# Two places in the order of a long fused kernel: when the sampling weights are loaded, and where a depthwise unit's closing activation stands

## The chip, the cores and the metric

The kernel runs on one core of one Trainium2 chip. The metric is the device time of one execution in microseconds (us). Of three runs of the kernel before, the median is 9661.97 us (9661.39 to 9698.82). The engines are TensorE (PE, with its weight loads as PEld), VectorE (DVE), ScalarE (ACT), GpSimd (POOL) and SyncE (SP, whose only work here is to issue DMAs).

## What is computed

The input is 32 images of 96 channels and 56 x 56 pixels, in float32. Two layers follow each other.

Layer 0 is an inverted bottleneck with quantised weights: a 1x1 convolution to 576 hidden channels, a 3x3 depthwise convolution, squeeze and excite, and a 1x1 convolution back to 96 channels, plus the input:

```python
h = silu(bn(conv1x1(x, fake_quant(w1)), g1, b1, m1, v1))
h = silu(bn(depthwise3x3(h, fake_quant(w2)), g2, b2, m2, v2))
pooled = mean(h, axis=(2, 3))
s = sigmoid(silu(pooled @ se_w1 + se_b1) @ se_w2 + se_b2)
x = x + bn(conv1x1(h * s, fake_quant(w3)), g3, b3, m3, v3)
```

Layer 1 attends and samples. It weighs its input by channel and by pixel from 2-D Fourier magnitudes, predicts nine offsets and a gate for each pixel by 3x3 convolutions, samples the weighted image bilinearly at the nine moved places, and normalises over the batch:

```python
y = x * ca * sa                              # from |rfft2(x)| and the mean and norm over channels
aux = concat([y, coord, resize(mean(|rfft2(y)|))])
offset, gate = conv3x3(aux), sigmoid(conv1x1(relu(conv3x3(aux))))
y_base = conv3x3(y)
sampled = bilinear(y, grid + offset)         # nine places a pixel, 0 outside
z = (1 - gate) * y_base + gate * einsum(sampled, def_w)
out = relu(batchnorm(z) + x)                 # statistics over all 32 images
```

## The kernel before

**The stages.** `layers` carries three things at once. The main loop goes over the 32 x 7 bands of layer 1 (a band is eight rows of an image; `bands`, L1073), and each band over two halves `h`. Beside it run two generators that belong to later images: `second` (`attend`, the end of layer 0 and the attention of layer 1 for the image after) and `first` (`hidden`, layer 0's expansion and depthwise part for the image after that). `pump` (L1012) is called between groups of matmuls and moves the generators on, each at a pace that brings it to its end with the image. There are seven pumps in a half and three more at a band's end. Work that is to follow later is put into the list `later` with the slot at which it is due.

**A depthwise unit.** `hidden` (L203) works on nine units of an image (`UNITS`: 128 hidden channels by half an image each). TensorE and ACT expand the unit after (L168, L172) while DVE runs the nine taps of this one into the accumulator `acch` (L259 for the first, L261 for the eight others). `acch` has two buffers. `finish` (L218) is the unit's end: a Silu with batchnorm as scale and bias, in place, which also sums over the pixels into `pooled` (L221), and a store of the result to `h2d` in DRAM from ACT's queue (L223). In the text `finish` of a unit is called after the fourth tap of the next unit (`n == 3`, L263). Unit 8's is put off with `defer` (L270): it becomes due with a flush when the image's generators are drained, right behind its last tap. The result is read back by `project_loads` (L305) for the projection matmuls L323 and L329.

**Sampling.** For each band `offsets` (a generator, moved on once before the halves and then at each pump) makes the offsets, stores them to DRAM (`od`, L655), loads them spread over the positions of a small neighbourhood (`ht`, L667, on SP), turns them into bilinear hat weights on ACT (L670, L671) and stores these (`hd`, L674, on ACT's queue). That is done two bands ahead. Each half of a band needs a weight tile, the product of a column part and a row part of `hd`. `weights_load` (L678) reads the two parts into `wc` (three buffers) and `wr` (two buffers) by four broadcasting DMAs of 252 KB each on SP, and `weights` (L690) multiplies them on DVE (L692). `sample_tiles` (L713) then multiplies blocks of the image (`yt`, made by `block_channels`, L696) with these weights on TensorE (L721), and ACT evicts the results into `v` (L725); `pack` moves a part of `v` to other partitions (L732), and `deform` is the convolution with `def_w` (L740).

In a half, the text has the order: `prepare` (the loads, L1117), the first group of samples with three pumps, the ends of the half before, the product of the weights for the next half (L1131), the second group with four pumps, `pack`. `prepare(upto)` issues loads until `upto` halves have theirs, as far as `hds` reaches. So a weight tile's loads are issued at the top of the half whose middle holds its product, and the tile is used in the half after that.

**What sets the order.** The instructions are written in one text, and a planner orders each engine's instructions ahead of time: it plays the program with estimated durations and puts an instruction into its engine's order when its inputs are there in that play. At run time an engine works its order from front to back and waits where an input is late. SP is left out of the planner (`manual_schedule`, L1351): its DMAs are issued in the order of the text. `tc.keep_in_program_order(ins)` gives the planner one more edge: `ins` comes after the instruction that the text has just before it on the same engine. It concerns the order alone and adds no wait. It is used once in the kernel before, at L670.

Of the kernel before, what the change touches and what calls it, by code (L numbers as in the profile page):

```python
# [9 lines left out]
AF = mybir.ActivationFunctionType  # L10
# [54 lines left out]
AHEAD = 1  # L65
READY = 1
# [50 lines left out]
def bank(p):  # L117
    return p["mm"].tile([128, 512], FP, name="mm")
# [33 lines left out]
def expand(nc, p, xts, unit):  # L152


    w = p["w0"]
    ch, half = unit
    h1 = p["hp"][p["n_hp"] % len(p["hp"])]
    p["n_hp"] += 1
    p["h1"] = h1
    inv, sh = w["inv1"][:, ch : ch + 1], w["sh1"][:, ch : ch + 1]  # L160
    w1 = w["w1"][:, ch * 128 : min(HID, ch * 128 + 128)]

    def piece(parts, row0, rows):

        pt = bank(p)
        for p0, hf in parts:
            r0 = row0 - 1 + hf
            nc.tensor.matmul(pt[p0 : p0 + w1.shape[1], : rows * W], w1, xts[hf][:, r0 * W : (r0 + rows) * W],  # L168
                             start=True, stop=True)
        lo = parts[0][0]  # L170
        hi = parts[-1][0] + w1.shape[1]
        nc.scalar.activation(h1[lo:hi, row0 : row0 + rows, 1 : 1 + W],  # L172
                             pt[lo:hi, : rows * W].rearrange("p (h w) -> p h w", h=rows), AF.Silu,
                             bias=sh[lo:hi], scale=inv[lo:hi])

    if half is None:
        nc.vector.memset(h1[:64, 0, :], 0.0)
        nc.vector.memset(h1[64:, HH + 1, :], 0.0)
        for r in range(1, HH + 1, ER):
            piece([(0, 0), (64, 1)], r, ER)  # L180
            yield
        piece([(0, 0)], HH + 1, 1)
        piece([(64, 1)], 0, 1)
        yield
    else:
        r = 1 - half
        for rows in (ER + 1, ER, ER, ER):
            piece([(0, half)], r, rows)
            r += rows
            yield  # L190
# [12 lines left out]
def hidden(tc, p, x, xn, h2d, pooled, defer):  # L203


    nc = tc.nc
    w = p["w0"]

    def rows_of(x, half):
        xt = p["xt"].tile([C, (HH + 1) * W], FP, name="xt")  # L210
        r0 = half * (HH - 1)
        nc.sync.dma_start(xt, x[:, r0 : r0 + HH + 1].rearrange("c h w -> c (h w)"))
        return xt

    xts = p.pop("xts", None) or [rows_of(x, 0), rows_of(x, 1)]
    for _ in expand(nc, p, xts, UNITS[0]):
        yield
    def finish(u, acc):  # L218
        ch = UNITS[u][0]
        flat = acc.rearrange("p h w -> p (h w)")  # L220
        nc.scalar.activation(flat, flat, AF.Silu, bias=w["sh2"][:, ch : ch + 1], scale=w["inv2"][:, ch : ch + 1],  # L221
                             accum_out=pooled[:, u : u + 1])
        nc.scalar.dma_start(h2d[u], flat)  # L223

    before = None
    for u, (ch, half) in enumerate(UNITS):
        h1 = p["h1"]
        more = expand(nc, p, xts, UNITS[u + 1]) if u + 1 < len(UNITS) else iter(())
        if xn is not None and u in (5, 8):

            p.setdefault("xts", []).append(rows_of(xn, int(u == 8)))
        acc = p["acch"].tile([128, HH, W], FP, name="acch")

        rows_of_tap = lambda dy: (int(half == 0 and dy == 0), HH - int(half == 1 and dy == 2))
        diag = p.get("diag")
        taps = [k for k in (4, 0, 1, 2, 3, 5, 6, 7, 8) if diag is None or k not in TPE]
        parts = []
        if diag is not None:
            for r0 in range(0, HH, ER):
                pt = bank(p)[:, :EW].rearrange("p (h w) -> p h w", h=ER)  # L240
                for i, k in enumerate(TPE):
                    dy, dx = divmod(k, 3)
                    lo, hi = rows_of_tap(dy)
                    lo, hi = max(r0, lo), min(r0 + ER, hi)
                    nc.tensor.matmul(pt[:, lo - r0 : hi - r0], diag[:, ch, i], h1[:, dy + lo : dy + hi, dx : dx + W],
                                     start=(i == 0), stop=(i == len(TPE) - 1))
                parts.append((slice(r0, r0 + ER), pt))
            next(more, None)
            yield
        for n, k in enumerate(taps):  # L250
            dy, dx = divmod(k, 3)
            lo, hi = rows_of_tap(dy)
            win = h1[:, dy + lo : dy + hi, dx : dx + W]
            wk = w["w2"][:, ch, k : k + 1]
            if n == 0:
                for rs, pt in parts:
                    nc.vector.scalar_tensor_tensor(acc[:, rs], win[:, rs], wk, pt, ALU.mult, ALU.add)
                if not parts:
                    nc.vector.tensor_scalar(acc, win, wk, None, ALU.mult)  # L259
            else:  # L260
                nc.vector.scalar_tensor_tensor(acc[:, lo:hi], win, wk, acc[:, lo:hi], ALU.mult, ALU.add)  # L261
            if n % 2:
                if n == 3 and before:  # L263
                    finish(u - 1, before)
                next(more, None)
                yield
        for _ in more:
            pass
        before = acc
    defer(lambda: finish(len(UNITS) - 1, before))  # L270


# [405 lines left out]
def weights_load(nc, p, hd, h):  # L678

    src = hd.rearrange("n i t k -> n i (t k)")[:, :, h * NTH * KP : (h + 1) * NTH * KP]  # L680
    wc = p["wc"].tile([2 * NS, NTH * KP], FP, name="wc")
    wr = p["wr"].tile([2 * NS, NTH * KP], FP, name="wr")
    for s in range(2):
        ps = slice(s * NS, (s + 1) * NS)
        nc.sync.dma_start(wc[ps], src[2 * s].unsqueeze(0).to_broadcast([SB, SB, NTH * KP]))
        nc.sync.dma_start(wr[ps], src[2 * s + 1].unsqueeze(1).to_broadcast([SB, SB, NTH * KP]))
    return wc, wr
# [251 lines left out]
def layers(tc, a, dp, x1d, zd, stats, far):  # L939
# [6 lines left out]
    nc = tc.nc  # L946
    B = x1d.shape[0]
    with ExitStack() as ctx:
# [143 lines left out]
        def prepare(upto):  # L1092

            nonlocal n_loads
            while n_loads < min(upto, 2 * len(hds)):
                n, m = divmod(n_loads, 2)
                loads.append(weights_load(nc, p, hds[n], m))
                n_loads += 1
# [6 lines left out]
        for n, (b, j) in enumerate(bands):  # L1105
            if j == 0:
                st = p["st"].tile([C, NBD, 6], FP, name="st")
            if j == turn:
                drain()
                refill(b + 1, j * RB - PD)  # L1110
                flush()
                start(b + 1, slots)
            more = find(n + 2) if n + 2 < len(bands) else iter(())
            next(more, None)
            for h in range(2):
                v = p["vp"].tile([128, NTAP, NTH, 2, TP], FP, name="v")
                prepare(2 * n + h + READY + AHEAD)  # L1117
                s = ready.pop(0)
                yt = yts.pop(0)
                for i, group in enumerate(GROUPS):  # L1120
                    sample_tiles(nc, p, yt, s, v, group)
                    for _ in range(group[0][0], group[-1][1]):
                        next(more, None)
                        pump()
                    if i == 0:
                        for end in ends:
                            end()
                        ends.clear()
                        if h == 1 and n + 1 < len(bands):
                            yts.append(block_channels(nc, p, yp, bands[n + 1][1], 0))  # L1130
                        ready.extend(weights(nc, *ws) for ws in loads[:1])  # L1131
                        del loads[:1]
                        if h == 0:
                            yts.append(block_channels(nc, p, yp, j, 1))
                pack(nc, v)
                if h == 0:
                    if n % 2 == 0:
                        gates.extend(gates_of(nc, p, hids[n // 2]))
                    gate = gates.pop(0)
                ends.append(lambda n=n, h=h, v=v, gate=gate, st=st: end_half(n, h, v, gate, st))  # L1140
            for _ in more:
                pass
            pump()
            pump()
            pump()
            if b + 1 < B:
                refill(b + 1, (j + 1) * RB - PD if j < NBD - 1 else H)
            if j == NBD - 1:
                nc.vector.tensor_reduce(top[:, NBD:], top, AX.X, ALU.max)
# [350 lines left out]
```

## Time and profile before

| | us |
|---|---|
| median of three runs | 9661.97 |
| profiled execution | 9648.5 |
| its span, first to last instruction | 9646.7 |
| PE busy | 8472.7 (88%) |
| DVE busy | 7227.2 (75%) |
| ACT busy | 5322.1 (55%) |
| POOL busy | 2532.6 (26%) |
| taps of the depthwise units on DVE (L261) | 4320.5 in 2250 instructions |
| products of the weights on DVE (L692) | 564.6 in 448 instructions |
| closing activations on ACT (L221) | 487.5 in 288 instructions |
| mean granted clock of TensorE | 0.923 |

The profile is one execution taken by the hardware profiler. A line of a group gives line, engine, operation, tiles (out<-in) and shapes. A line of the waits reads "who <- for whom: total us, times, longest". A line of the timeline gives start, duration, engine (with a q: its queue, which issues DMAs), line, operation, tiles, count, and in square brackets the engine's idle time before it with what ended it. A line of a table of windows gives the window, its length, the busy time and count of each engine, the clock that was granted to TensorE (1 is full speed), the share of the DMA engines' time and GB/s.

### The profile page before, as it was taken

How to read it: one execution, taken by the hardware profiler on the slowest of the kernel's cores; microseconds unless marked ns; L12 is line 12 of the kernel's file. 1: busy time of each engine (PE TensorE's matmuls, PEld its weight loads, DVE VectorE, ACT ScalarE, POOL GpSimd, SP SyncE). 2: the span in 40 equal slices, each digit the busy share in tenths (PEclk: the TensorE clock that was granted, in tenths of full speed). 3: DMA queues.
4: the chain of work that ended last, by engine and by line, in shares of the span. 5: the costliest groups of instructions: out<-in, count | busy, mean ns of one | idle time of the engine just before them, and what ended most of it. 6: DMA issues, size and time to landing. Idle time of an engine off the chain costs nothing. (4 is left out here: it accounts for less than half of the span.)

```text
span 9646.7 us, 129705 instructions
## 1 busy us (share of the span) xinstructions
PE 8472.7 (88%) x48374; PEld 5064.2 (52%) x48374; DVE 7227.2 (75%) x6948; ACT 5322.1 (55%) x10262; POOL 2532.6 (26%) x2642
## 2 busy tenths in 40 slices
PE   6889989998999999999899989999999999999870
PEld 3455555555555555555555555555555555555540
DVE  7688777778777787877777887777878777777323
ACT  2355555565555556555555655555555555565453
POOL 1123223222222322222232322233222323322210
PEclk9899999999999999999999999999999999999985
DMA  2355555555555555555555555555555555554449
GB/s 94 95 143 148 151 152 160 150 149 143 147 155 154 160 154 145 145 149 155 154 160 155 145 142 153 151 158 154 153 139 145 150 157 157 153 152 135 130 154 417
DMA packets 1069473, 1485.98 MB, mean 154 GB/s; under 512 B 590438, under 2 KB 840086, under 8 KB 1056550
## 3 DMA queue, kind: packets, MB, share of 16 engines
q1 hardware_dynamic: 858747, 985.20, 37.9%
q10 hardware_dynamic: 153803, 329.80, 9.2%
q0 software_dynamic: 56288, 162.60, 6.7%
q8 instruction: 388, 6.36, 0.3%
q14 instruction: 247, 2.02, 0.1%
HBM read 1064.29 MB, written 412.65 MB: 153 GB/s over the span
## 5 line engine op out<-in xcount | busy, mean ns | idle before, releaser
L261 DVE SCALAR_TENSOR_TENSOR acch<-hp,w,acch 128x1512 f32<-128x1512 f32 (+1 forms) x2250 | 4320.5, 1920 | 32.8
L605 PE MATMUL mm<-yp,c_jointW 104*128 104x448 f32 x4032 | 1649.0, 561 | 9.0 <-ACT yt L709 5.5
L740 PE MATMUL pd<-v,c_def 128*96 128x224 f32 (+1 forms) x6272 | 1414.8, 376 | 127.6 <-ACT v L732 104.1
L703 POOL COPY ybl<-yp 96x448 f32<-96x448 f32 x896 | 1014.7, 1159 | 1903.7 <-PE mm L707 1903.3
L721 PE MATMUL mm<-wc,yt 64*96 64x144 f32 x12544 | 1168.1, 308 | 153.5 <-DVE yb L638 76.8
L740 PEld LDWEIGHTS pd<-v,c_def 128*96 128x96 f32 (+1 forms) x6272 | 1051.8, 173 | 437.4 <-ACT v L732 142.5
L168 PE MATMUL mm<-xt,w 96*128 96x392 f32 (+3 forms) x2688 | 1136.3, 561 | 133.8 <-ACT yt L709 96.0
L605 PEld LDWEIGHTS mm<-yp,c_jointW 104*128 104x128 f32 x4032 | 783.6, 196 | 806.0 <-issue 762.6
L721 PEld LDWEIGHTS mm<-wc,yt 64*96 64x96 f32 x12544 | 884.2, 167 | 489.8 <-issue 188.0
L221 ACT ACTIVATE acch<-acch,sh,inv 128x1568 f32<-128x1568 f32 x288 | 487.5, 1693 | 1159.0 <-DVE acch L261 1143.9
L692 DVE TENSOR_TENSOR wc<-wc,wr 128x1008 f32<-128x1008 f32 x448 | 564.6, 1260 | 704.2 <-DMA wr<-hd 690.5
L725 ACT COPY v<-mm 96x288 f32<-96x288 f32 (+1 forms) x2688 | 1003.6, 442 | 117.7 <-PE mm L721 78.9
L172 ACT ACTIVATE hp<-mm,sh,inv 128x392 f32<-128x392 f32 (+2 forms) x1216 | 811.8, 672 | 326.9 <-PE mm L168 282.1
L633 PE MATMUL mm<-yp,c_base0W 96*64 96x448 f32 x4032 | 913.5, 550 | 0.0
L323 PE MATMUL mm<-hq,w3s 128*96 128x392 f32 x2048 | 788.2, 531 | 127.4 <-DMA hq<-h2d 125.9
L655 POOL DMA_DIRECT2D od<-at x224 | 186.3, 832 | 2275.1 <-DVE at L651 1451.9
L732 ACT COPY v<-v 32x448 f32<-32x448 f32 x1344 | 755.3, 562 | 30.3
L168 PEld LDWEIGHTS mm<-xt,w 96*128 96x128 f32 (+1 forms) x2688 | 389.9, 189 | 495.1 <-issue 264.8
L709 ACT COPY yt<-mm 128x384 f32<-128x384 f32 (+1 forms) x896 | 350.9, 441 | 491.5 <-PE mm L707 489.4
L323 PEld LDWEIGHTS mm<-hq,w3s 128*96 128x96 f32 x2048 | 336.3, 173 | 477.7 <-issue 382.5
L466 POOL TENSOR_TENSOR o<-o,xc 96x392 f32<-96x392 f32 x256 | 396.5, 1549 | 643.9 <-ACT o L333 642.3
L633 PEld LDWEIGHTS mm<-yp,c_base0W 96*64 96x64 f32 x4032 | 294.6, 134 | 515.5 <-issue 490.2
(194 smaller groups left out, 9023.7 us busy)
## 6 DMA issues: line engine op xcount, KB each, us to landing
h2d<-acch ACTq DMA_DIRECT2D x288, 784.0 KB
wc<-hd SPq DMA_DIRECT2D x896, 252.0 KB
wr<-hd SPq DMA_DIRECT2D x896, 252.0 KB
hq<-h2d SPq DMA_DIRECT2D x128, 980.0 KB
hq<-h2d SPq DMA_DIRECT2D x128, 784.0 KB
x<-x1d SPq DMA_DIRECT2D x768, 98.0 KB
ht<-od SPq DMA_DIRECT2D x224, 252.0 KB
hd<-ht ACTq DMA_DIRECT2D x224, 252.0 KB
```

What stands on the lines that cost most here:

```text
L168: nc.tensor.matmul(pt[p0 : p0 + w1.shape[1], : rows * W], w1, xts[hf][:, r0 * W : (r0 + rows) * W], start=True, stop=True)
L172: nc.scalar.activation(h1[lo:hi, row0 : row0 + rows, 1 : 1 + W], pt[lo:hi, : rows * W].rearrange("p (h w) -> p h w", h=rows), AF.Silu, bia ...
L261: nc.vector.scalar_tensor_tensor(acc[:, lo:hi], win, wk, acc[:, lo:hi], ALU.mult, ALU.add)
L323: nc.tensor.matmul(pts[half][:C, :EW], w3s[:, ch], hq, start=(i == 0), stop=False)
L605: nc.tensor.matmul(view, weights[:, k], yp[:channels, r0 : r0 + RB, dx + PD - 1 : dx + PD - 1 + W], start=(k == 0), stop=(k == NTAP - 1))
L633: nc.tensor.matmul(pb[k % 2 * BC : (k % 2 + 1) * BC, :BW].rearrange("p (h w) -> p h w", h=RB), w["base"][:, k], yp[:C, r0 : r0 + RB, dx + ...
L692: nc.vector.tensor_tensor(wc, wc, wr, ALU.mult)
L703: nc.gpsimd.tensor_copy(yb[:, :, s], blocks)
L721: nc.tensor.matmul(pt[k][:C, (t - lo) * KP : (t - lo + 1) * KP], yt[ps, t], s[ps, t * KP : (t + 1) * KP], start=True, stop=True)
L725: nc.scalar.copy(v[:C, :, lo:hi, k].rearrange("c k t p -> c t k p"), pt[k][:C, : (hi - lo) * KP].rearrange("c (t k p) -> c t k p", t=hi - ...
L732: nc.scalar.copy(v[C:, 1 + 2 * i : 3 + 2 * i], v[i * QC : (i + 1) * QC, KA:])
L740: nc.tensor.matmul(out.rearrange("c q (t x) -> c t q x", x=TS), p["w"]["def"][ks, k], v[ks, k].rearrange("c t s (r x) -> c t (s r) x", r=T ...
```

## The change

The closing activation of a depthwise unit (L221) is wrapped in `tc.keep_in_program_order`. And `prepare`, which issues the loads of the weights, moves from the top of a half to just behind the product of the weights in its middle, with an argument that is larger by one: a weight tile's four loads are now issued half a half ahead of where they were, behind the product of the tile before it. The instructions themselves, the buffers and their sizes are the same.

```diff
     def finish(u, acc):
         ch = UNITS[u][0]
         flat = acc.rearrange("p h w -> p (h w)")
-        nc.scalar.activation(flat, flat, AF.Silu, bias=w["sh2"][:, ch : ch + 1], scale=w["inv2"][:, ch : ch + 1],
-                             accum_out=pooled[:, u : u + 1])
+        tc.keep_in_program_order(nc.scalar.activation(
+            flat, flat, AF.Silu, bias=w["sh2"][:, ch : ch + 1], scale=w["inv2"][:, ch : ch + 1], accum_out=pooled[:, u : u + 1]))
         nc.scalar.dma_start(h2d[u], flat)
...
             for h in range(2):
                 v = p["vp"].tile([128, NTAP, NTH, 2, TP], FP, name="v")
-                prepare(2 * n + h + READY + AHEAD)
                 s = ready.pop(0)
                 yt = yts.pop(0)
                 for i, group in enumerate(GROUPS):
...
                         ready.extend(weights(nc, *ws) for ws in loads[:1])
                         del loads[:1]
+                        prepare(2 * n + h + 1 + READY + AHEAD)
                         if h == 0:
                             yts.append(block_channels(nc, p, yp, j, 1))
```

## The prediction

> **What bounds the kernel now.** I read the page's busy shares first, then a table of windows over the long middle stage, then the waits, then the timeline around one wait of each kind.
>
> ```profile
> PE 8472.7 (88%) x48374; PEld 5064.2 (52%) x48374; DVE 7227.2 (75%) x6948; ACT 5322.1 (55%) x10262; POOL 2532.6 (26%) x2642
> ...
> 480.00:9120.00 8640.00, 7923.65 (x45735) 4738.19 (x45738) 6739.73 (x6242) 4956.84 (x9646) 2441.68 (x2507) 0.94 0.54 150
> ...
> ACT acch L221 <- DVE acch L261: 1143.9, 185, 12.7
> ...
> DVE wc L692 <- DMA wr<-hd: 690.5, 152, 18.3
> ...
> PE mm L323 <- DMA hq<-h2d: 125.9, 31, 9.4
> ...
> PE pd L740 <- ACT v L732: 104.1, 84, 5.4
> ```
>
> In the middle stage (480 to 9120 us, its columns being PE, PEld, DVE, ACT, POOL, clock, DMA share, GB/s) TensorE works 7923.65 of 8640 us: it is the bound, with 716 us idle. The clock row says 0.94; it is 1 or 0.5, so 6% of 8640 = 518 us of full clock are lost too. Idle time of ACT and DVE counts only where TensorE ends up waiting for it.
>
> **Who makes TensorE idle.** I followed each of its idle stretches between 500 and 8800 us (684 us together) back through the instruction that released it and the ones ahead of that on its engine, until TensorE or a DMA was met. 203 us of it lead through a wait of ACT at L221, 227 us through a wait of DVE at L692, 61 us of these through both; 116 us end at the hq loads, 64 us at the ht load. One L221 case:
>
> ```profile
> 4035.62 1.69 ACT L221 ACTIVATE acch<-acch,sh,inv 128x1568 f32<-128x1568 f32 x1 [4.98 <-DVE acch L261]
> ...
> 4037.22 0.19 ACT L221 ACTIVATION_READ_ACCUMULATOR acch<-acch,sh,inv 128x1 f32 x1
> 4037.31 0.49 ACT L725 COPY v<-mm 96x432 f32<-96x432 f32 x1
> ...
> 4037.71 0.51 ACT L725 COPY v<-mm 96x432 f32<-96x432 f32 x1
> 4037.86 0.24 PEld L721 LDWEIGHTS mm<-wc,yt 64*96 64x96 f32 x2 [1.85 <-ACT v L725]
> ```
>
> ACT stands 4.98 us in front of the unit's last tap with two evictions (L725) queued behind it, and TensorE then waits 1.85 us for a bank that these would have freed.
>
> **The pin, step by step.** In the trace L221 starts 0.04 us after the unit's ninth tap in nearly all units, though in the text it stands after four taps of the next unit (17.5 us later on the mean over 262 units). So it floats ahead of its text place. The pin puts it behind the ACT instruction written just before it. I found that instruction by walking the generators' steps in the text, and its end in the trace. By unit 0 to 8 of an image it ends 15.9, 27.2, 22.6, 19.1, 12.4, 6.3, 13.0, 17.1 and -8.8 us after today's start of L221 (medians). Sorted by the same units, the waits of 29 images are 302, 158, 121, 1, 0, 0, 138, 139 and 221 us. In units 0, 1, 2, 6 and 7 the data is there long before the new place: 857 us of ACT waiting go. Unit 8 is finished straight after its last tap in the text as well, so its 221 us stay; no TensorE stretch leads to them. All of the 203 us lead to the units that move.
>
> The instruction count does not change: 288 x (1.69 + 0.19 us) of ACT and 288 stores. The store (L223, 784 KB) moves with L221, on ACT's own queue; its packets in the trace end 2.9 to 9.6 us after issue. Who needs it: the tap L259 two units on, which reuses the buffer. Today's start of that tap, less new place, 2.4 us of ACT and the store's own time, leaves 9 us or more, but a median of 2.1 us in unit 1 and 1.9 us in unit 4. A DVE that runs ahead of today's pace by more waits there.
>
> What I take: two thirds of 203 us, 135 us, because another reason then ends part of those stretches (bounds 0 and 203). The clock: per idle microsecond 518/716 = 0.72 us are lost to it; I take half of 0.72 x 135, 49 us (bounds 0 and 146). Sum for the pin: -184 us, between 0 and -349.
>
> The clock by windows:
>
> ```profile
> 4036.00:4042.00 6.00, 4.33 (x32) 3.15 (x31) 3.87 (x4) 5.94 (x14) 3.79 (x5) 1.00 0.85 242
> ...
> 4244.00:4248.00 4.00, 1.96 (x18) 1.32 (x16) 3.91 (x3) 3.95 (x5) 2.83 (x2) 1.00 0.00 0
> 4248.00:4252.00 4.00, 1.84 (x5) 0.91 (x6) 4.00 (x3) 3.94 (x11) 0.00 (x0) 0.69 0.00 0
> 4252.00:4256.00 4.00, 4.00 (x6) 1.75 (x6) 4.00 (x5) 3.83 (x7) 0.00 (x0) 0.50 0.23 62
> ```
>
> One short stretch leaves the clock at 1.00; two windows only half busy, in which no stretch is over 2.03 us, bring 0.69 and 0.50. So several short stretches close together cost clock, and a removed one may save some. The Trainium skill ("TensorE: Matmul & The Clock Gate", Part 1: The HAM clock gate) says that the clock halves after an idle window of about 3.4 us. Read as one unbroken gap that rule would strike my 49 us and make the sum -135; the row contradicts that reading, and I go by the row.
>
> A rule that speaks against the pin: the Trainium skill ("ScalarE: Activation LUTs", What ACT_TABLE_LOAD costs) puts a change of function table at 1283 ns plus a drain of about 1380 ns, and unit 3's Silu now lands next to the square roots. Two more changes an image would be 2 x 30 x 2.66 = 160 us of ACT by the page. By the row (ACT_TABLE_LOAD 1283 ns, 62 of them at L417) they are 77 us of ACT. But L479, unit 3's predecessor, stands after L478's root and before the L172 that reloads the Silu table already, so the load only moves there: 0, bounds 0 and 77 us, in units where ACT is 57% busy.
>
> **The loads, step by step.** Each group is four DMAs on SP's queue (0.57 to 0.60 us of issue each, 2.4 us), in the order of the text. It moves from the top of a half to just behind the preceding product, ahead of what the four pumps after the second group of samples, the pack and a band's end put on SP: up to six x loads (L361), two hq loads (L305), yp rows (L584, L596), an xt load (L212). Its floor is the latest of: the issue before it on SP, the hd store, the last product on its wr buffer, the last L721 on its wc buffer. By today's times of these, of the 14 groups of an image ten go out 3 to 21 us earlier (mean over all 14, 9 us) and four do not move (0 to 0.7 us), since there SP stood behind one of those already. Where it now waits for hd, what stands behind it is held: an xt load 22 us (needed units later), the first hq load up to 8.8 us (the next one waits 15 us for the h2d store anyway, and its matmul comes 29 us on), x loads 7 us (read 16 us later). I cost this at 0.
>
> Does it remove DVE's waits? The dearest are not moved:
>
> ```profile
> 4228.15 0.58 SPq L685 DMA_DIRECT2D wc<-hd  x1
> ...
> 4230.08 0.58 SPq L686 DMA_DIRECT2D wr<-hd  x1
> ...
> 4240.81 1.21 DVE L692 TENSOR_TENSOR wc<-wc,wr 128x1008 f32<-128x1008 f32 x1 [4.86 <-DMA wr<-hd]
> 4241.94 0.63 DVE L414 TENSOR_TENSOR s<-sq 128x464 f32<-128x464 f32 x1
> ...
> 4242.67 1.00 ACT L413 ACTIVATE sq<-mm 128x464 f32<-128x464 f32 x2 [4.73 <-DVE s L414]
> ```
>
> This product comes some 34 us before its first matmul and holds L414, ACT and then TensorE: 168 us of waits in 29 images, 163 us of TensorE's idle time. Its load waits for a wc buffer and for the ht load ahead of it, which the change leaves ahead. The waits at places that do move (68, 95 and 172 us) reach TensorE in 55 us, nearly all shared with L221 and counted there. A load that lands earlier also lets the product be queued earlier on DVE, in front of taps and L414, with a wait of the same kind. So the loads count 0, bounds +326 (two new places like this one) and -163 (this one goes).
>
> **Sum.** The profiled execution is 9648.5 us (span 9646.7). 9648.5 - 184 = 9465; the median of the runs, 9662, lies 13.5 us above the profiled one, and I say 9470, about 2.0% less than the median.
>
> **Rivals.** (a) Products queued too early: as just told, 163 us a place. It needs (184 + 48)/163 = 1.4 such places to be slower by 0.5%; two give 9648.5 - 184 + 326 = 9790. For it: loads now run further ahead at ten places. Against: five places have early loads today, and only one of them makes DVE wait. (b) The freed ACT time is caught by the next wait (hq, ht, DVE's late L638), or the pinned place brings back the float: 9650. For it: 315 of 684 us of idle do not pass L221's or L692's waits. Against: the two L725 behind L221 depend on nothing later. (c) The accumulator buffer: 60 waits of 3 us in units 1 and 4, 180 us of DVE, half of it on TensorE: 9560. (d) The product at 4240.81 also stops waiting because everything ahead of it shifts: 9648.5 - 184 - 163 = 9300.
>
> **Chances.** A run of this kernel tells 0.5% (48 us) from no change. Forecast 0.52, (c) 0.08 and (d) 0.15 make faster 0.75; (b) 0.13 is same; (a) 0.12 slower. The range runs from (d), less 10 for the clock, to past (b) into the near part of (a): 9290 to 9700.
>
> **What would show it.** Right: the wait of ACT at L221 falls from 1143.9 to about 290 us, L221 starts after the next unit's taps, TensorE's idle time in the middle stage falls from 716 to near 580 us and the clock rises above 0.94. Wrong: DVE's wait at L692 grows past 690.5 us with TensorE behind it (a), L259 waits for the h2d store (c), or more ACT_TABLE_LOADs.

## The result, and the profile after

| | before | after |
|---|---|---|
| median of the runs, us | 9676.99 (9661.39 to 9698.82, 4 runs) | 10003.56 (9976.76 to 10020.29, 4 runs) |
| ratio, 95% interval | | 1.0333 [1.0298, 1.0368] |
| span of the profiled execution | 9646.7 | 10007.5 |
| PE busy | 8472.7 | 8730.4 |
| PE idle (span less busy) | 1174.0 | 1277.1 |
| mean granted clock of TensorE | 0.923 | 0.901 |

The change makes the kernel 3.3% slower, where 2% faster was forecast. First the page's busy line and the middle stage in the table of windows (length; busy time and count of PE, PEld, DVE, ACT, POOL; granted clock; DMA share; GB/s), both of the kernel after.

```profile
span 10007.5 us, 129802 instructions
...
PE 8730.4 (87%) x48374; PEld 5217.7 (52%) x48374; DVE 7258.5 (73%) x6948; ACT 5324.1 (53%) x10264; POOL 2582.9 (26%) x2642
...
480.00:9120.00 8640.00, 7850.32 (x43810) 4689.04 (x43808) 6587.74 (x6034) 4774.42 (x9270) 2398.95 (x2402) 0.91 0.54 145
```

The same 48374 matmuls take 258 us more, and TensorE idles 103 us more; the two make up the 361 us of span. So most of the loss isn't waiting but matmuls at the slower clock, and the question is what brought that clock about. In the middle stage TensorE's idle time, forecast to fall from 716 to near 580 us, rose to 790, and the clock, forecast to rise, fell from 0.94 to 0.91. The waits, in the kernel after:

```profile
DVE wc L692 <- DMA wr<-hd: 930.5, 238, 20.5
...
ACT yb L628 <- DVE at L651: 536.3, 128, 7.5
...
PE mm L721 <- DVE yb L638: 321.0, 108, 8.4
...
DVE yb L638 <- ACT yb L636: 297.0, 98, 6.8
...
ACT acch L221 <- DVE acch L261: 221.5, 32, 8.7
...
PE pd L740 <- ACT v L732: 54.3, 93, 1.4
```

Three of the same in the kernel before, and ACT's wait for the ht load, which is needed further on:

```profile
ACT yb L628 <- DVE at L651: 128.0, 70, 5.2
PE mm L721 <- DVE yb L638: 76.8, 55, 6.1
DVE yb L638 <- ACT yb L636: 116.8, 41, 6.1
...
ACT ht L670 <- DMA ht<-od: 79.2, 50, 4.5
```

ACT's wait at L221 went as forecast (1143.9 to 221.5 us). But DVE's wait for the weights' loads grew from 690.5 us in 152 waits to 930.5 in 238, ACT's wait at L628 for DVE from 128.0 to 536.3, and TensorE's at L721 for L638 from 76.8 to 321.0. How they hang together is seen in one stretch of the timeline, kernel after:

```profile
997.78 0.57 SPq L686 DMA_DIRECT2D wr<-hd  x1
...
1008.39 1.21 DVE L692 TENSOR_TENSOR wc<-wc,wr 128x1008 f32<-128x1008 f32 x1 [6.50 <-DMA wr<-hd]
...
1009.64 0.69 DVE L651 COPY at<-mm 18x224 f32<-18x224 f32 x2
...
1010.36 0.63 ACT L628 ACTIVATE yb<-mm,c_cvec 32x448 f32<-32x448 f32 x1 [5.99 <-DVE at L651]
...
1011.04 0.48 PE L721 MATMUL mm<-wc,yt 64*96 64x144 f32 x2 [1.43 <-ACT yb L628]
...
1012.28 0.62 DVE L638 TENSOR_TENSOR yb<-yb,mm 64x448 f32<-64x448 f32 x1 [1.32 <-ACT yb L636]
```

The last of the four loads goes out at 997.78. DVE is at the product already at 1001.89 and stands there 6.50 us. Behind it stands L651, for which ACT waits 5.99 us, and for what ACT then frees TensorE waits 1.43 us. What that costs is in the windows around it, kernel after, same columns as above:

```profile
1005.00:1010.00 5.00, 4.61 (x25) 1.92 (x21) 1.57 (x3) 0.00 (x0) 0.00 (x0) 1.00 0.90 255
1010.00:1015.00 5.00, 3.25 (x19) 2.25 (x20) 1.56 (x4) 4.40 (x11) 1.90 (x3) 0.75 0.62 163
1015.00:1020.00 5.00, 5.00 (x18) 3.13 (x18) 0.99 (x3) 2.67 (x6) 0.00 (x0) 0.50 0.69 237
1020.00:1025.00 5.00, 5.00 (x26) 3.73 (x25) 1.27 (x2) 2.76 (x5) 0.00 (x0) 0.73 0.50 139
```

TensorE is idle for 0.39 + 1.75 us in the first two of them, and then the clock is at 0.75, 0.50 and 0.73 of full: 5 x (0.25 + 0.50 + 0.27) = 5.1 us of work at full clock are lost, more than twice the idle time. Between 500 and 8800 us the clock stood at half for 1031 us before and for 1464 us after. I sorted these stretches by the idle time in the 7 us ahead of each: where most of that leads through a wait of DVE at L692, alone or with L221's, they make up 478 us before and 935 us after. That is more than the whole growth of 433 us. It sorts by what stood ahead and doesn't yet show a cause: what goes when that wait goes, the runs with the product tied have to tell.

The product is in fact early. Paired with the first matmul that reads it, it starts 14.7 us ahead of it before (median) and 29.5 us after. Tied to its place in the text (the runs e6 and e3 below) it starts 12.6 us ahead with the loads where they were and 16.4 us with the loads moved. So the planner had it only some 2 us early before and has it 13 us early after: the loads are issued earlier, so in the planner's play the data is there earlier, and the product is put further forward in DVE's order than the data really comes.

### The profile page after: what moved, and what is told of

The parts are those of the page before. It is cut to its first block, busy times and chain, and to the rows that moved or that the text cites. A ratio compares the mean times of both kernels' runs of the same rounds, so it can differ in the third digit from the quotient of the medians.

```text
span 10007.5 us, 129802 instructions
## 1 busy us (share of the span) xinstructions
PE 8730.4 (87%) x48374; PEld 5217.7 (52%) x48374; DVE 7258.5 (73%) x6948; ACT 5324.1 (53%) x10264; POOL 2582.9 (26%) x2642
## 5 line engine op out<-in xcount | busy, mean ns | idle before, releaser
L605 PE MATMUL mm<-yp,c_jointW 104*128 104x448 f32 x4032 | 1687.3, 571 | 6.7 <-DMA yp<-fqd 5.0
L721 PE MATMUL mm<-wc,yt 64*96 64x144 f32 x12544 | 1243.8, 320 | 406.5 <-DVE yb L638 321.0
L703 POOL COPY ybl<-yp 96x448 f32<-96x448 f32 x896 | 978.4, 1119 | 2076.7 <-PE mm L707 2076.2
L740 PE MATMUL pd<-v,c_def 128*96 128x224 f32 (+1 forms) x6272 | 1437.1, 379 | 83.3 <-ACT v L732 54.3
L721 PEld LDWEIGHTS mm<-wc,yt 64*96 64x96 f32 x12544 | 954.7, 176 | 782.0 <-DVE yb L638 349.5
L692 DVE TENSOR_TENSOR wc<-wc,wr 128x1008 f32<-128x1008 f32 x448 | 561.6, 1254 | 1007.4 <-DMA wr<-hd 930.5
L168 PE MATMUL mm<-xt,w 96*128 96x392 f32 (+3 forms) x2688 | 1195.0, 581 | 91.2 <-ACT yt L709 56.1
L740 PEld LDWEIGHTS pd<-v,c_def 128*96 128x96 f32 (+1 forms) x6272 | 1063.5, 176 | 403.9 <-issue 104.8
L172 ACT ACTIVATE hp<-mm,sh,inv 128x392 f32<-128x392 f32 (+2 forms) x1216 | 810.9, 671 | 412.2 <-PE mm L168 350.4
L323 PE MATMUL mm<-hq,w3s 128*96 128x392 f32 x2048 | 749.9, 510 | 45.3 <-DMA hq<-h2d 42.4
L732 ACT COPY v<-v 32x448 f32<-32x448 f32 x1344 | 755.2, 562 | 29.6
L625 ACT ACTIVATE hid<-mm,c_dg1b 50x448 f32<-50x448 f32 x224 | 140.6, 628 | 999.5 <-PE mm L605 991.0
L386 PE MATMUL mm<-c_FU,x 112*128 112x116 f32 x3072 | 495.9, 313 | 128.2 <-POOL x L366 99.2
L221 ACT ACTIVATE acch<-acch,sh,inv 128x1568 f32<-128x1568 f32 x288 | 488.2, 1695 | 223.6 <-DVE acch L261 221.5
L386 PEld LDWEIGHTS mm<-c_FU,x 112*128 112x128 f32 x3072 | 458.2, 222 | 270.6 <-POOL x L366 135.6
```

Of the source, the lines that this page charges most:

```text
L323: nc.tensor.matmul(pts[half][:C, :EW], w3s[:, ch], hq, start=(i == 0), stop=False)
L386: nc.tensor.matmul(pt[:, i * 4 * V : (i + 1) * 4 * V], x2s[g][:, 2 * i : 2 * i + 2, :].rearrange("h c w -> h (c w)"), w["FU"], start=True, ...
L605: nc.tensor.matmul(view, weights[:, k], yp[:channels, r0 : r0 + RB, dx + PD - 1 : dx + PD - 1 + W], start=(k == 0), stop=(k == NTAP - 1))
L703: nc.gpsimd.tensor_copy(yb[:, :, s], blocks)
L721: nc.tensor.matmul(pt[k][:C, (t - lo) * KP : (t - lo + 1) * KP], yt[ps, t], s[ps, t * KP : (t + 1) * KP], start=True, stop=True)
L732: nc.scalar.copy(v[C:, 1 + 2 * i : 3 + 2 * i], v[i * QC : (i + 1) * QC, KA:])
```

## The experiments

Every run is compared with the kernel before, run on the same chip beside it. The theories in the quoted expectations: **P**, the product goes too early into DVE's order. **A**, the activation's new place does the harm. **S**, SP stands in its order in front of the hd store and holds what is behind. **H**, the time that the pin frees on ACT is caught at the ht load. Others are explained where they come up.

### The two parts alone

e1 has the change's first hunk only, e2 the second only:

```diff
# e1
+        tc.keep_in_program_order(nc.scalar.activation(
+            flat, flat, AF.Silu, bias=w["sh2"][:, ch : ch + 1], scale=w["inv2"][:, ch : ch + 1], accum_out=pooled[:, u : u + 1]))
# e2
-                prepare(2 * n + h + READY + AHEAD)
...
+                        prepare(2 * n + h + 1 + READY + AHEAD)
```

> The pin alone, with the loads where they were before. Theory P (product): the loss comes from the moved loads, which let the planner queue the weight products earlier on DVE, where they wait in front of other work; the pin itself gains what was forecast for it in part: 9480 to 9640 us, DVE's wait at L692 near the 690 us of before, ACT's at L221 near 220. Theory A (activation): the later Silu is what costs: near 10000 us. Theory S (SP queue): as P here, the loads on SP being what costs.

> The loads moved alone, the activation free as before. Theory P: about 9950 to 10200 us, DVE's wait at L692 900 us or more, products some 30 us ahead of their first matmul. Theory A: near 9660 us. Theory S: about 10000 us too, with SP's wait for hd near 1590 us (703 before).

Measured: e1 1.0011 [0.9996, 1.0026], no change; e2 1.0179 [1.0157, 1.0202]. The loads' move does harm by itself, and more with the pin (1.0333 / 1.0011 = 1.032). No theory had e2's time, 9837 us: it lies under the forecasts of P and S and over that of A, and its products start 28.7 us ahead of their matmuls, as P said, though DVE's wait for their loads is 734.1 us and not 900. The pin gives nothing though it takes away the wait it was to take away. In the waits of e1:

```profile
ACT ht L670 <- DMA ht<-od: 254.5, 108, 7.5
...
ACT acch L221 <- DVE acch L261: 247.3, 32, 9.0
...
PE pd L740 <- ACT v L732: 222.2, 66, 8.1
```

L221 waits 247.3 us where it waited 1143.9, but L670's wait for the ht load rose from 79.2 to 254.5 us, and TensorE's at L740 for ACT's L732 from 104.1 to 222.2. One case in the timeline of e1:

```profile
1365.08 0.57 SPq L686 DMA_DIRECT2D wr<-hd  x1
1365.76 0.66 SPq L667 DMA_DIRECT2D ht<-od  x1
...
1376.26 0.77 ACT L670 ACTIVATE ht<-ht,c_blk 112x576 f32<-112x576 f32 x1 [5.51 <-DMA ht<-od]
...
1379.19 1.15 ACT L732 COPY v<-v 32x448 f32<-32x448 f32 x2
...
1379.81 3.30 PE L740 MATMUL pd<-v,c_def 128*96 128x224 f32 x8 [6.15 <-ACT v L732]
```

The ht load goes out at 1365.76 behind four weight loads and is there at 1376.26, 10.5 us after issue. ACT, no longer held at L221, comes to L670 earlier, stands there 5.51 us with the copies of `pack` (L732) behind it, and TensorE loses 6.15 us. Traced back, the idle time of TensorE that ends at the ht load is 64 us before and 219 us in e1; that through L221's wait went from 203 to 0.

### The product tied to its place in the text

```diff
-def weights(nc, wc, wr):
+def weights(nc, wc, wr, tc=None):
-    nc.vector.tensor_tensor(wc, wc, wr, ALU.mult)
+    m = nc.vector.tensor_tensor(wc, wc, wr, ALU.mult)
+    if tc is not None:
+        tc.keep_in_program_order(m)
...
-                        ready.extend(weights(nc, *ws) for ws in loads[:1])
+                        ready.extend(weights(nc, *ws, tc) for ws in loads[:1])
```

e3 has it on the change whole, e4 on the pin alone, e6 on the kernel before, e7 on the loads' move alone. In these kernels lines behind L692 stand two further (L721 is L723).

> Both parts of the change, and the product of the weights (L692) also tied to its place in the text. The loads on SP stay as early as in the changed kernel. Theory P: products return to some 15 us ahead of their first matmul, DVE's wait at L692 falls below 250 us and the time to 9400 to 9600 us. Theory A: near 10000 us. Theory S: SP's wait for hd stays near 1590 us and the time above 9900 us.

> The activation and the product tied, the loads where they were before. Theory P: the one early product of before (168 us of waits an execution) goes, late loads stay: L692 waits 300 to 500 us, 9450 to 9620 us, not faster than with the earlier loads. Theory S: faster than with the moved loads by 300 us or more. Theory A: near 10000 us.

> The product of the weights tied alone; neither part of the change. If the early product of before costs what its chain showed (163 us of TensorE's idle time), 9480 to 9560 us. If the tie helps only together with the pin, 9620 us or more, since ACT's 1144 us of waits at L221 stay.

> The loads moved and the product tied, the activation free. If the product's early place is what the moved loads cost, the step from the loads alone (9837) is as large as the one from the changed kernel to both and tied (10004 to 9584, 420 us): 9420 to 9560 us. If the loss was an interplay with the pin, less: 9650 to 9800 us.

Measured, with the eight kernels as pairs:

| | product free | product tied | tied / free |
|---|---|---|---|
| neither part | 1 | e6 0.9765 [0.9747, 0.9783] | 0.977 |
| pin | e1 1.0011 | e4 0.9798 [0.9779, 0.9818] | 0.979 |
| loads | e2 1.0179 | e7 0.9960 [0.9941, 0.9978] | 0.978 |
| both | after 1.0333 | e3 0.9905 [0.9878, 0.9931] | 0.959 |

Four lines in `weights` take 4.1% off the changed kernel, so the product's place is the largest single price paid there. But the same lines take 2.1 to 2.4% off the other three, the kernel before among them: it paid most of this already. In the waits of e3:

```profile
PE mm L723 <- DVE yb L638: 290.6, 81, 6.6
...
DVE wc L692 <- DMA wr<-hd: 216.5, 53, 9.6
```

DVE's wait at the product falls from 930.5 to 216.5 us. TensorE's wait for L638, which I had thought to be its measure, falls only from 321.0 to 290.6: it names the last releaser and not the root. The idle time that leads back through L692's waits does fall, from 376 to 138 us, and the half clock behind such idle time from 935 to 430 us. In all, the half clock falls by less, from 1464 to 1181 us, since other waits then stand ahead of more of it.

Theory P is not all of it. By the same table the loads' move still costs 2.0% with the product tied (e6 to e7) and 1.1% on top of the pin (e4 to e3); for e4 theory P had expected no gain over e3.

What belongs to the change is the difference of two such steps. Without the pin the move costs 1.8% with the product free and 2.0% with it tied, so there the product's place explains none of its cost. e7's 9627 us lies between the two forecasts made for it, nearer to the one for an interplay with the pin (9650 to 9800) than to the one for the product's place (9420 to 9560). With the pin the move costs 3.2% with the product free and 1.1% with it tied. The whole change costs 1.4% with the product tied (0.9905 / 0.9765) instead of 3.3%: about 1.9 points of it go with the product's place, in company with the pin, and 1.4 do not. Nor does the size of the wait tell the price. DVE's wait at the product in e2, e7 and e6:

```profile
DVE wc L692 <- DMA wr<-hd: 734.1, 221, 20.7
...
DVE wc L692 <- DMA wr<-hd: 176.4, 45, 8.3
...
DVE wc L692 <- DMA wr<-hd: 419.8, 88, 18.4
```

From e2 to e7 it loses 558 us and the time falls by 2.15%; from the kernel before to e6 it loses 271 us and the time falls by 2.35%.

### The hat activations one pump later

```diff
-    for _ in range(6):
+    for _ in range(7):
         yield
     p["tc"].keep_in_program_order(nc.scalar.activation(ht, ht, AF.Abs, bias=w["blk"]))
     nc.scalar.activation(ht, ht, AF.Relu, bias=w["one"], scale=-1.0)
-    yield
```

e5 has it with the pin, e8 with pin and tied product, e12 with the tied product alone.

> The pin alone, and the two activations on ht (L670, L671) one pump later, behind the half's last evictions and pack. Theory H (ht): what the pin freed was caught by ACT's wait for the ht load (79 us before, 255 with the pin alone), which holds the pack and so TensorE. Then that wait falls below 80 us, TensorE's wait at L740 for L732 from 222 to near 60 us, and the time to 9480 to 9600 us. Rival theory D (DVE): the gain was caught by DVE's wait at L692 (884 us with the pin alone): the time stays within 40 us of the pin alone, 9640 to 9700.

> Activation and product tied, loads where they were before, the ht activations one pump later. Theory H: faster than the same without the last part (9468) by 60 to 150 us: 9320 to 9410 us. Theory D or none: 9450 to 9490 us.

> Product tied, loads where they were before, ht activations one pump later, activation L221 free: the fastest version so far (9429) without its pin. If the pin is worth something once the wait for ht is out of its way, 9470 to 9560 us; if it is worth nothing, 9400 to 9450 us.

Measured: e5 0.9939 [0.9923, 0.9956], against e1's 1.0011; e8 0.9735 [0.9719, 0.9751], against e4's 0.9798; e12 0.9756 [0.9739, 0.9772], against e6's 0.9765. The pair with the pin gains 0.6 to 0.7%, the pair without it 0.1%, within the intervals. So the ht load did catch part of what the pin freed, though less of it than theory H gave for e5 and e8 (9625 us against 9480 to 9600, 9429 against 9320 to 9410). The wait itself doesn't shrink (286.8 us in e5, 296.8 in e8); what changes is who stands behind it. TensorE's wait at `deform` for L732 goes from 211.5 us in e4 to 8.3 in e8, and its idle time that ends at the ht load from 200 to 42 us.

But with the hat activations later the pin is worth 0.2% (e12 to e8), again within the intervals: of 203 us of idle time that led through it, next to nothing comes back as time. In e5 the next to catch it are DVE's products, with 181 us of idle time that ends at the loads of the weights.

### Which of the moved groups costs

A band has two groups of loads. In e9 only the second half's is moved, in e10 only the first half's, both with the product tied; e11 is e9's order with the pin and a free product. In e9 and e11 `if h == 1:`, in e10 `if h == 0:` stands ahead of both calls:

```diff
-                prepare(2 * n + h + READY + AHEAD)
+                if h == 1:
+                    prepare(2 * n + h + READY + AHEAD)
...
+                        if h == 1:
+                            prepare(2 * n + h + 1 + READY + AHEAD)
```

> Product tied, activation free, and only every second group of loads moved: the second half's of a band, whose hd was stored a band earlier. The first half's stays at the top of its half. With the product tied the kernel takes 9456 us with no group moved and 9627 with all moved. Theory S (SP's wait for hd, 518 against 1588 us): the groups moved here find hd stored, SP's wait stays below 800 us and the time is 9440 to 9510 us. Rival theory B (bunching of the loads, or their earlier traffic): about half of the loss or more, 9540 to 9650 us.

> The other half of the move: only the groups of a band's first half, which follow the hd store by three pumps in the text, go behind the product. Theory S: SP's wait for hd near 1500 us and most of the loss: 9580 to 9650 us. Theory B: half of the loss or less, 9480 to 9560 us.

> The changed kernel (activation tied, product free) with only the second half's groups moved. If the loss of 3.3% is the early product (as tying it there gave back 4.2%) and the early product follows from every moved group: about half of the loss or more, 9820 to 9960 us. If the wait for hd is the larger part: 9680 to 9780 us.

Measured: e9 1.0408 [1.039, 1.0425], e10 0.9973 [0.9959, 0.9987], e11 1.0555 [1.0533, 1.0578]. Theory S was right for e10 (the first half's group is the one that follows the hd store: SP waits 1790 us for hd, and the cost is the whole 2%) and plainly wrong for e9, where SP waits 527 us as in e6 (518) and the kernel is 6.6% slower than e6. Moving one of the two brings both groups into one half, which moving both does not. In e9 a wait stands out that is 14.0 us in e6:

```profile
PE acc L284 <- ACT acch L221: 204.2, 31, 10.7
```

e11's 10212 us is over both of its forecasts too. So these runs price another order rather than take apart the first.

### The distance to the hd store

Still open was whether SP's order explains the 2% from e6 to e7. e13 is e7 with the hd store two pumps earlier in the text. e14 is e7 with the loads two pumps later. e15 is e6 with the rest of the offsets' steps behind the band's last three pumps.

```diff
# e13
-    for _ in range(6):
+    for _ in range(4):
         yield
...
     hds.append(hd)
+    for _ in range(2):
+        yield
# e14
-                        prepare(2 * n + h + 1 + READY + AHEAD)
...
-                    for _ in range(group[0][0], group[-1][1]):
+                    for k in range(group[0][0], group[-1][1]):
                         next(more, None)
                         pump()
+                        if k == 4:
+                            prepare(2 * n + h + 1 + READY + AHEAD)
# e15
-            for _ in more:
-                pass
             pump()
             pump()
             pump()
+            for _ in more:
+                pass
```

> Loads moved, product tied to its place (as in the run e7, 9627 us), and the two hat activations and the hd store made two pumps earlier, so that the first moved group stands eight pumps behind its hd store instead of six (ten in e6, where the loads are not moved). Theory S (the moved loads cost because SP, in order, stands in front of hd and holds the x loads behind it, whose readers GpSimd L366 and TensorE L386 then stop): SP's wait for hd at L685 falls from 1588 us to 700 to 1200, the waits of TensorE for POOL's x at L388 fall from 332 us to under 150, and the time from 9627 to 9500 to 9570. Theory Q (the cost is that four loads of 252 KB now stand in another place of the queues and land beside other transfers, wherever hd is): hd wait falls, time stays 9600 to 9650.

> As e7 (product tied, 9627 us), but the loads are issued two pumps behind the product's place, that is halfway between the place of the change and the old one. Theory S: the group stands eight pumps behind its hd store, SP's wait for hd falls from 1588 us to 700 to 1200, the time to 9500 to 9570, between e7 and e6 (9456). Theory Q: the place matters and not hd: anything from 9400 to 9700, not tied to the hd wait; it would not go with the result of the run with hd made earlier.

> Loads where they were, product tied (as in the run e6, 9456 us), but the rest of the offsets' steps, with the hat activations and the hd store, is taken behind the band's three last pumps instead of in front of them: the first group that needs the hd stands seven pumps behind its store instead of ten. Theory S: SP's wait for hd rises from 518 us to 1000 to 1500 though no load has moved, TensorE's waits for POOL's x grow, and the time rises to 9530 to 9620. Theory Q: the time stays within 0.5% of 9456.

(The L388 in the first expectation is a slip for L386.)

Measured: e13 0.9925 [0.9896, 0.9954], e14 0.9748 [0.9724, 0.9772], e15 0.9776 [0.9757, 0.9796]. e13 and e15 hardly moved what they were to move: L670 starts 15.6 us behind the issue of the ht load instead of 16.9 in e13, and SP's wait for hd is 1523 us instead of 1588 there and 526 instead of 518 in e15. The store's real place comes from its inputs and the planner, so these two tell little. e14 tells more. Two pumps are enough to take off the whole 2%, though SP still waits twice as long for hd as in e6. The wait in e14 and in e6:

```profile
SPq L685 <- DMA hd<-ht: 1092.0, 153, 20.4
...
SPq L685 <- DMA hd<-ht: 517.7, 42, 20.8
```

A wait of SP's is thus not by itself the cost. And what theory S needed, x loads that come late, isn't there. In e7, the view of GpSimd's line L366 (what it waited for, and who waited for it: us, times):

```profile
its engine sat idle before it (us, times) until:
  DMA x<-x1d: 4.4, 1
who waited for it (us, times):
  PEld mm L386: 336.1, 66
  PE mm L386: 285.5, 50
```

L366, which multiplies the loaded x for TensorE's L386, waits 4.4 us for its load and still makes TensorE wait 285.5 us; in e14 that is 105.8.

### The store of z tied to its place

Followed back on GpSimd, 281 us of TensorE's waits in e7 lead through L366 to what stands ahead of it there: 159 us to the store of z (L1048), waiting for DVE, and 107 us to the sab load (L586). In e6 these are 82 and 31. Theory **G**: it is GpSimd's order.

```diff
         def store(b, j, z):
-            nc.gpsimd.dma_start(zd[b][:, j * BW : (j + 1) * BW], z)
+            tc.keep_in_program_order(nc.gpsimd.dma_start(zd[b][:, j * BW : (j + 1) * BW], z))
```

> Loads moved, product tied (as e7, 9627 us), and the store of z (L1048, on GpSimd's queue) tied to its place in the text too, seven pumps behind the combination it stores. Theory G (the rest of the cost of the moved loads is GpSimd's order: in e7, 281 us of TensorE's waits lead to the product x by sa on GpSimd, L366, which is not late by its own load (4.4 us of waiting) but stands behind the store of z, 159 us, and the load of sab, 107 us; in e6 these are 82 and 31): the 159 us go, TensorE's waits for L366 fall from 286 to under 150 us, and the time from 9627 to 9480 to 9550. Theory S (SP's wait for hd, now 1588 us, holds what is behind it): SP's order is not touched, the time stays 9600 to 9650.

> Product tied, loads where they were (as e6, 9456 us), and the store of z tied to its place. Theory G: 82 us of TensorE's waits lead through this store in e6, so 9370 to 9440, and the distance to the run before (e7's 170 us) falls to under 110. Theory S: 9440 to 9470, and the distance stays near 170 us.

> The fastest version so far (activation and product tied, hat activations a pump later; 9429 us) with the store of z tied too. Theory G: 9350 to 9415. Theory S: 9415 to 9445.

Measured: e16 0.9989 [0.9976, 1.0002], e17 0.9808 [0.979, 0.9826], e18 0.9767 [0.975, 0.9783]. Nothing is gained (in medians 9638.6, 9467.6 and 9424.4 us against 9627, 9456 and 9429 without the edge). In e16 the way through the store of z is still 170 us: z itself comes late from DVE. Theory G falls in this form. What remains of the loads' move, 1 to 2% with the product tied, is shown, without the pin, to hang on those two pumps and not on late x loads or the place of z's store. Its root isn't settled, and neither is why the product's place counts in the move's cost only together with the pin.

The lowest ratio measured is that of e8 (pin, product tied, hat activations a pump later, loads where they were), 0.9735 of the kernel before; e14 with 0.9748 and e12 with 0.9756 are within the intervals of it. The change's place for the loads has no part in it, and the pin hardly any.

## Why the prediction was wrong

**What bounds the kernel.** TensorE does, and of the chains followed back the one through L692 (227 us) mattered; but the working took its places as given, 163 us at the product at 4240.81 and 55 us at others, which it counted with L221. Tying all of them was worth 2.35% by the ratio, 9674 to 9456 us in the medians, and in the profiled executions 97 us of idle time and 101 us of PE time. That could have been tried as the first question: why is a product that needs no hurry standing in front of DVE's work at all?

**The pin.** Its mechanism was right: the wait at L221 fell to 247 us alone and 221.5 with the loads (about 290 forecast), and L221 now starts 16.5 us behind its unit's last tap on the mean. So were the points meant to cost nothing. There are 133 table loads where there were 131, with 30 moved from L172 to L221, and L259 waits once, 6.2 us, for the store of `acch` (rival (c) needed 60 times 3 us). The step that failed is "two thirds of 203 us, 135 us, because another reason then ends part of those stretches": the other reasons took the place of all of it (TensorE's idle time between 500 and 8800 us is 738 us in e1, 684 before). For the pin alone rival (b) was right, with the very wait it named, ht.

**The clock.** "I take half of 0.72 x 135, 49 us" priced an idle microsecond at 0.36 us of clock. From before to after it was 258/103 = 2.5 us, and from before to e6, with 101 us of PE time and 97 us of idle time less, 1.0. The reading that short stretches close together cost clock held; but a price per idle microsecond does not carry from kernel to kernel. In e1, TensorE idles 58 us more than before and works 21 us less.

**The loads.** This decided the result. "So the loads count 0" failed: alone they cost 1.8%, 174 us. Rival (a) had the mechanism of a part of it, that a load which lands earlier lets the product be queued earlier on DVE with a wait of the same kind, and set it aside with "five places have early loads today, and only one of them makes DVE wait". That counted the waits at the places as they were, while the planner chooses these places anew from the loads' new times. DVE's waits at L692 rose by 86 in number and 240 us in length, and the products went from 14.7 to 29.5 us ahead of their use. Tying them took 419 us off (10003.6 to 9584.1), but it took 218 us off the kernel before as well (9674.4 to 9456.3), so some 200 us of the loss belong to this mechanism, and only with the pin beside the loads: for the loads alone it is not what the 1.8% are made of. The other part, "what stands behind it is held ... I cost this at 0", isn't decided: something of 1 to 2% is there with the product tied, and the runs have not shown that it is SP's queue.

**The range.** Its top, 9700, reached only into the near part of (a), whose own figure was 9790; with the pin worth nothing, the 326 us of (a) on the 9648.5 of the profiled execution make 9975, near the 10004 measured. That nearness is luck: 326 us were two places at 163 us, and what came is some 200 us by the products and the rest by something that the prediction had at nothing.

## What to carry to other kernels

Where a planner orders an engine by the time at which data should be there, an earlier load is not only an earlier load: it moves its consumer forward too, and an in-order engine then stands there with everything behind it. Tie a consumer that has slack to its place before its loads are moved, and price a removed wait by what the engine meets next in its order. When a cure helps the changed kernel, try it on the kernel before too: only the difference belongs to the change. Where TensorE's busy time changes at an equal count of matmuls, look at the clock before looking for work.

## What the runs showed of the hardware

- Idle time in small pieces can cost more clock than its length, as in the windows from 1005 to 1025 us (2.1 us idle, 5.1 us of clock lost). In the kernel after, between 500 and 8800 us, the clock went to half 188 times, but only 46 idle stretches were as long as 3.4 us (before: 148 and 42). The pin alone has 94 such stretches and less half clock than after (1134 us against 1464). The Trainium skill ("TensorE: Matmul & The Clock Gate", Part 1: The HAM clock gate) gives one idle window of about 3.4 us as the cause of the half clock; read as one unbroken stretch, that would explain at most a quarter of these.
- The half clock goes with TensorE's idle share of one step of the clock. In the clock's records of these traces the clock changes only on a fixed grid of 3.41 us. Between 500 and 8800 us, after a step at full clock in which TensorE sat idle for 60% or more, in one piece or several, the next step was at half clock in 94 of 94 cases after and 86 of 86 before; at 50 to 60% in 38 of 40 and 21 of 25; at 40 to 50% in 41 of 60 and 13 of 34; below 30% in 6 of 1746 and 8 of 1931. So the same idle time costs clock or none by how it falls into these steps.
- The ht load, issued right behind four 252 KB loads on the same queue, took 10.5 us to its reader in e1, and the last weight load of the example after, issued at 997.78, 10.6 us to 1008.39.
